# Scores and maxima of a whole chunk interleaved, and attention values summed chunk by chunk

## The chip, the cores and the metric

The kernel runs on one core of one Trainium2 chip. The metric is the device time of one execution in microseconds. Before the change three runs took 3262.71, 3264.76 and 3274.87 us; the median is 3264.76.

## The reference

Two transformer layers of the same form are applied to `x` of 4 sequences of 512 rows and 320 columns, with a context of 4 sequences of 1601 rows and 192 columns. Each layer normalises, does self-attention with 20 heads of 16 columns, normalises, does cross-attention to the context, normalises, and ends with a gated feed-forward part of 1280 hidden columns. Everything is fp32.

```python
def _attn(x, ctx, wq, wk, wv, wo, bo, heads):
    q = (x @ wq).reshape(b, n, heads, dh).transpose(0, 2, 1, 3)
    k = (ctx @ wk).reshape(b, j, heads, dh).transpose(0, 2, 1, 3)
    v = (ctx @ wv).reshape(b, j, heads, dh).transpose(0, 2, 1, 3)
    sim = jnp.einsum('bhid,bhjd->bhij', q, k) * scale
    a = jax.nn.softmax(sim, axis=-1)
    out = jnp.einsum('bhij,bhjd->bhid', a, v)
    return out.transpose(0, 2, 1, 3).reshape(b, n, heads * dh) @ wo + bo
...
x = _attn(h1, h1, ...) + x          # self: 512 keys
x = _attn(h2, context, ...) + x     # cross: 1601 keys
ff = a * jax.nn.gelu(g, approximate=False) @ ff_w2 + ff_b2
```

## The kernel before

**Units.** Attention is cut into units: one layer, one kind (self or cross), one sequence and one group of four heads. There are 20 self units and then 20 cross units in each layer, followed by four feed-forward units. A unit goes over its keys in chunks of 128: 4 chunks in a self unit, 13 in a cross unit (the last has 65 keys). So there are 160 self chunks and 520 cross chunks.

**Work of one chunk.** For each of the four heads `score` makes the transposed scores, 128 keys by 512 queries, in one PSUM bank `st`, in three passes: two products of 32 rows (queries split in a high and a low part; line 1113) and a product of 2 rows that subtracts each query's maximum (line 1116). Head j uses rows 32j to 32j+31 of TensorE, a row tile; products on different row tiles run side by side. ScalarE (ACT) then takes the exponential out of the bank into SBUF (line 1126).

**Maxima.** The maxima of a unit have to be known before its scores, so the products for them (`sps`, line 926) are made one unit ahead and stand beside the scores of the current unit: while heads 0 and 1 are scored, the maxima of heads 2 and 3 are made on the two free row tiles, and then the other way round. A bank pair holds 128 queries by 512 keys of two heads, and VectorE (DVE) reduces it (line 947). The last 65 keys of a cross unit go as a remainder of eight small passes per half (line 969). A chunk thus has two halves. `round_of` issues one half: pass by pass, the scores first, then the maxima. `give` hands out the maxima for a half; some halves get none, and some chunks get further rounds of maxima alone.

**Values.** `values` multiplies the exponentials by the values of the chunk, four heads on four column tiles (`av`, line 1141; a column of ones beside the values makes the sums). It is issued one chunk late, after the scores of the next chunk. A self unit does this for each chunk. A cross unit does it for two chunks at a time, accumulated in one bank (`n = 2 if u.cross else 1`). ACT copies the bank to SBUF (line 1157) and GpSimd (POOL) adds it to `o` (line 1158); the first copy of a unit goes straight to `o` (line 1152). The last unit before a feed-forward part has no maxima to make; it scores all four heads in one round, and there DVE adds the bank to `o` (line 1154).

**Order.** The program writes the order of each engine's queue itself. After the scores, and the late values, `steps` takes pending work from chains, by due times and a credit that each half (`tick`) adds to: query projections (line 717), keys of the context (line 779), values of the context (line 869), output projections (line 1050), normalisations. Banks come from two rings: `st`, four banks, for scores, values and most projections, and `m`, two double banks, for maxima. The exponentials and the copies of values go to SBUF places that are taken in turn (`place`, 10 in self units and 13 in cross units).

Of the kernel before, what the change touches and what calls it, by code (L numbers as in the profile page):

```python
# [64 lines left out]
def kernel(ctx: ExitStack, tc: tile.TileContext, x, context, ws, out):  # L65
# [97 lines left out]
    def place():  # L163
        these = places[at_place["kind"]]
        at_place["i"] = (at_place["i"] + 1) % len(these)
        return these[at_place["i"]]
# [184 lines left out]
    def pick():  # L351
        heads = [
            (q[0][1] + late_by(n), n)
            for n, q in chains.items()
            if q and q[0][2]() and q[0][3]() and (q[0][0][0] != LIGHT or clock["lights"])
        ]
        return min(heads)[1] if heads else None

    def run(chain):
        costs, _, ready, _, f = chains[chain].popleft()  # L360
        assert ready(), chain
        f()
        clock["credit"] -= sum(costs)
# [15 lines left out]
    def next_cost():  # L379
        name = pick()  # L380
        return None if name is None else sum(chains[name][0][0])

    def tick():
        clock["round"] += 1
        clock["credit"] = max(-2.0, min(4.0, clock["credit"] + pace()))

    def steps(beside, lights=1):


        tick()  # L390
        clock["lights"], clock["slots"] = lights, 4
        clock["tiles"] = True if beside is None else None
        done = 0
        while True:
            name = pick()
            if name is None:
                break
            cost = sum(chains[name][0][0])
            if cost >= 0.1:
                share = (2.2, 1.1) if beside else (9.0, 9.0) if beside is False else (0.5, 0.75, 1.5)  # L400
                least = cost * share[done] if done < len(share) else 3.0
                if clock["credit"] < (3.0 if beside is False else least):
                    break
                done += 1
                if clock["tiles"] is not None:
                    clock["tiles"] = name in ALIKE
            run(name)
            if cost == LIGHT:
                clock["lights"] -= 1
            clock["slots"] -= name == "slots"  # L410
        clock["tiles"] = None

    def until(test, name):
        while not test():
            assert chains[name], name
            run(name)
# [570 lines left out]
    def max_reduce(u):  # L987
        if u.pm is not None:
            nc.vector.tensor_reduce(
                u.nm.rearrange("p (j t) -> p t j", t=NQ), u.pm, AX.X, ALU.max, negate=True  # L990
            )
# [91 lines left out]
    def flush():  # L1083
        for f in late:
            f()
        late.clear()

    def round_of(scores, maxima):

        todo = [f() for f in scores] + [f() for f in maxima]  # L1090
        for i in range(max((len(passes) for passes, _ in todo), default=0)):
            for passes, _ in todo:
                if i < len(passes):
                    passes[i]()
        for _, then in todo:
            then()

    def main(u, give, nxt):

        pr = {}  # L1100
        if at_place["kind"] != u.kind:
            at_place.update(kind=u.kind, i=min(at_place["i"], len(mine) - 1))

        def score(c, j, st=None):
            r = min(P, u.nkeys - c * P)
            rows = slice(j * SLOT, (j + 1) * SLOT)
            if st is None:
                st = ps_st.tile([P, N], F32, tag="st", name="st")
            keys = u.kT[rows, u.k0 + u.cols[c] : u.k0 + u.cols[c] + r].bitcast(F32R)
            two_rows = slice(j * SLOT, j * SLOT + 2)  # L1110

            def product(e):
                nc.tensor.matmul(st[:r, :], lhsT=keys, rhs=u.q[rows, e, :].bitcast(F32R), start=(e == 0), stop=False)  # L1113

            def less_maximum():
                nc.tensor.matmul(  # L1116
                    st[:r, :],
                    lhsT=units_of[two_rows, :r].bitcast(F32R),
                    rhs=u.mrow[two_rows, :].bitcast(F32R),
                    start=False,  # L1120
                    stop=True,
                )

            def exponential():
                p = place()
                nc.scalar.activation(p[:r], st[:r], AF.Exp)  # L1126
                pr[c, j] = p

            return [lambda: product(0), lambda: product(1), less_maximum], exponential

        last = nxt is None or nxt.kind == "ff"

        def values(cs):
            if u.g in (0, 2):
                until(lambda: units[u.i - u.g].vmade[u.g // 2] > cs[-1], "values")
            ps = ps_st.tile([P, N], F32, tag="st", name="av")
            for c in cs:
                r = min(P, u.nkeys - c * P)
                for j in range(HG):
                    head = (c * H + u.g * HG + j) * VW  # L1140
                    nc.tensor.matmul(  # L1141
                        ps[j * SLOT : (j + 1) * SLOT, :],
                        lhsT=columns_of[:r, head : head + SLOT],
                        rhs=pr.pop((c, j))[:r, :],
                        start=(c == cs[0]),
                        stop=(c == cs[-1]),
                    )
            u.valued = cs[-1] + 1

            if cs[0] == 0:  # L1150
                u.o = three.tile([P, N], F32, tag="o", name="o")
                (nc.vector.tensor_copy if last else nc.scalar.copy)(u.o, ps)
            elif last:
                nc.vector.tensor_tensor(u.o, ps, u.o, ALU.add)
            else:
                vo = place()
                nc.scalar.copy(vo, ps)  # L1157
                nc.gpsimd.tensor_tensor(u.o, u.o, vo, ALU.add)  # L1158
            if u.valued == u.nch:
                add_finish(u)  # L1160


        n = 2 if u.cross else 1
        together = {min(c + n, u.nch) - 1: list(range(c, min(c + n, u.nch))) for c in range(0, u.nch, n)}

        for c in range(u.nch):
            extra = []
            if last:

                both = ps_m.tile([P, 2, N], F32, tag="m", name="st")  # L1170
                round_of([lambda j=j: score(c, j, both[:, j % 2] if j > 1 else None) for j in range(HG)], [])
                tick()
            else:
                for odd in range(2):
                    if odd:
                        tick()
                    pair, rounds = give(2 * c + odd)
                    extra += rounds
                    round_of([lambda j=j: score(c, j) for j in ((2, 3) if odd else (0, 1))], pair)
            u.scored = c + 1  # L1180

            start["both"] = True
            if extra:
                round_of([], extra[0])
            start["both"] = False
            flush()
            if c in together:
                late.append(lambda cs=together[c]: values(cs))
            steps(None, 1 if extra or c == u.nch - 1 else 2)
            for i, e in enumerate(extra[1:]):  # L1190
                if i and next_cost() is not None:
                    run(pick())
                start["both"] = True
                round_of([], e)
                start["both"] = False
            if not last and c == u.nch - 3:
                max_reduce(nxt)
                max_end(nxt)
            if loads:
                loads.popleft()()  # L1200
# [232 lines left out]
    first = units[0]  # L1433
# [22 lines left out]
    for i, u in enumerate(units):  # L1456
        nxt = units[i + 1] if i + 1 < len(units) else None
        before(u)
        if u.kind == "ff":

            flush()
            now(loads)
            loads.clear()
            until(lambda: u.hT is not None, "norm")
        add_norms(i)
        start["both"] = u.kind == "ff"
        for k in (3, AHEAD):
            v = units[i + k] if i + k < len(units) else None
            if v is not None and v.kind != "ff" and v.early == (k == AHEAD):
                add_proj(v)  # L1470
                if v.g == 0:
                    add_values(v)
        (ff_main if u.kind == "ff" else main)(u, giver(u), nxt)
# [27 lines left out]
```

## Time and profile before

| What | us |
|---|---|
| median of three runs | 3264.76 |
| profiled execution, its own time | 3267.39 |
| span of the profiled execution | 3265.6 |
| DVE, reductions for maxima `pm` (line 947) | 1127.6 busy, 980 times |
| ACT, exponentials to `pr` and `wself` (line 1126) | 947.1 and 427.6 busy |
| ACT, copies of values to `pr` (line 1157) | 140.9 busy, 236 times |
| POOL, additions of `pr` to `o` (line 1158) | 302.2 busy, 236 times |

Busy time is the union of the instructions' times on the engine. A wait is put down to the engine whose signal came last. PE is the matmul stream of TensorE, PEld its weight loads; their ends are modelled. The granted clock of TensorE was 0.967 of full speed over the span.

### The profile page before, as it was taken

How to read it: one execution, taken by the hardware profiler on the slowest of the kernel's cores; microseconds unless marked ns; L12 is line 12 of the kernel's file. 1: busy time of each engine (PE TensorE's matmuls, PEld its weight loads, DVE VectorE, ACT ScalarE, POOL GpSimd, SP SyncE). 2: the span in 40 equal slices, each digit the busy share in tenths (PEclk: the TensorE clock that was granted, in tenths of full speed). 3: DMA queues.
4: the chain of work that ended last, by engine and by line, in shares of the span. 5: the costliest groups of instructions: out<-in, count | busy, mean ns of one | idle time of the engine just before them, and what ended most of it. 6: DMA issues, size and time to landing. Idle time of an engine off the chain costs nothing.

```text
span 3265.6 us, 89144 instructions
## 1 busy us (share of the span) xinstructions
PE 3117.7 (95%) x36690; PEld 1686.7 (52%) x36690; DVE 2077.9 (64%) x2833; ACT 1866.6 (57%) x3721; POOL 972.6 (30%) x1141
## 2 busy tenths in 40 slices
PE   7899899999999999999998998999999999999999
PEld 3455455555455555455444554555555555554555
DVE  6766777777777776522246777777777777774221
ACT  3666566776667676711126665667767777765110
POOL 2435232323323332111114453324233333322000
PEclk8999899999999999999989998999999999999999
DMA  3433222211212211200113332212112111112000
GB/s 92 91 65 77 44 43 45 54 39 38 65 33 42 60 35 28 80 4 6 27 23 73 72 62 44 41 40 51 33 39 55 36 41 39 39 22 65 9 10 15
DMA packets 213039, 145.08 MB, mean 44 GB/s; under 512 B 65556, under 2 KB 203160, under 8 KB 212632
## 3 DMA queue, kind: packets, MB, share of 16 engines
q1 hardware_dynamic: 211368, 138.32, 19.1%
q8 instruction: 289, 4.73, 0.6%
q10 hardware_dynamic: 1264, 1.06, 0.1%
q14 instruction: 118, 0.97, 0.1%
HBM read 33.04 MB, written 7.93 MB: 13 GB/s over the span
## 4 chain that ended last, share of the span: by engine, by line
PE 80%; DVE 8%; ACT 4%; issue 3%; DMA 2%; SPq 2%; POOL 1%; ACTq 0%; DVEq 0%; POOLq 0%
PE av L1141 19%; PE st L1113 19%; PE fps L1246 9%; PE st L1116 6%; PE yps L1302 5%; PE sps L926 5%; DVE pm L947 3%; PE kps L779 3%; PE qps L717 3%; PE vps L869 3%; PE ops L1050 3%; DVE nmax L947 2%; PE fps L1259 2%; ACT pr L1126 2%; PE kps L749 1%
## 5 line engine op out<-in xcount | busy, mean ns | idle before, releaser
L947 DVE TENSOR_REDUCE pm<-sps 128x2 f32<-128x1024 f32 (+1 forms) x980 | 1127.6, 1195 | 225.3 <-PE sps L926 199.6
L1113 PE MATMUL st<-q,kT 32*128 32x512 f32 (+1 forms) x5440 | 1089.3, 445 | 40.5 <-DVE x L1057 8.0
L1126 ACT ACTIVATE pr<-st 128x512 f32<-128x512 f32 (+1 forms) x1791 | 947.1, 602 | 269.9 <-PE st L1116 252.1
L926 PE MATMUL sps<-kT,q 32*128 32x512 f32 (+1 forms) x6400 | 993.6, 411 | 52.9 <-DMA kT<-stage 20.1
L1113 PEld LDWEIGHTS st<-q,kT 32*128 32x128 f32 (+1 forms) x5440 | 537.6, 182 | 482.3 <-ACT pr L1126 160.2
L1116 PE MATMUL st<-m,units 2*128 2x512 f32 (+1 forms) x2720 | 655.3, 400 | 5.9 <-issue 2.1
L1141 PE MATMUL av<-pr,vals 128*32 128x512 f32 (+1 forms) x3582 | 644.5, 636 | 16.9 <-ACT pr L1126 10.3
L1158 POOL TENSOR_TENSOR o<-o,pr 128x512 f32<-128x512 f32 x236 | 302.2, 1281 | 951.2 <-ACT pr L1157 931.2
L926 PEld LDWEIGHTS sps<-kT,q 32*128 32x128 f32 x6400 | 474.1, 188 | 103.6 <-DVE pm L947 33.3
L947 DVE TENSOR_REDUCE nmax<-sps 128x2 f32<-128x1024 f32 (+1 forms) x356 | 381.2, 1109 | 175.2 <-PE sps L926 121.6
L1126 ACT ACTIVATE wself<-st 128x512 f32<-128x512 f32 (+1 forms) x801 | 427.6, 602 | 75.1 <-PE st L1116 68.6
L1116 PEld LDWEIGHTS st<-m,units 2*128 2x128 f32 (+1 forms) x2720 | 350.7, 184 | 42.8 <-issue 7.7
L1141 PE MATMUL av<-wself,vals 128*32 128x512 f32 (+1 forms) x1602 | 344.5, 635 | 3.6 <-ACT pr L1126 3.0
L1246 PE MATMUL fps<-hT,w 128*128 128x512 f32 x640 | 285.4, 599 | 1.8 <-DVE pr L1272 0.9
L1269 ACT ACTIVATE pr<-fps,b 128x512 f32<-128x512 f32 x80 | 50.6, 683 | 370.4 <-PE fps L1259 268.1
L1141 PEld LDWEIGHTS av<-pr,vals 128*32 128x32 f32 (+1 forms) x3582 | 114.3, 112 | 236.9 <-issue 101.4
L1158 POOL TENSOR_TENSOR o<-o,wself 128x512 f32<-128x512 f32 x89 | 114.0, 1281 | 381.5 <-ACT wself L1157 381.5
L1157 ACT COPY pr<-av 128x512 f32<-128x512 f32 x236 | 140.9, 597 | 135.7 <-PE av L1141 134.7
L1246 PEld LDWEIGHTS fps<-hT,w 128*128 128x128 f32 x640 | 118.9, 190 | 151.8 <-issue 146.6
L624 POOL TENSOR_SCALAR stage<-stage 128x256 fp32r<-128x256 f32 (+1 forms) x155 | 107.1, 691 | 218.6 <-ACT stage L725 135.5
L624 POOL TENSOR_SCALAR w<-w 128x896 fp32r<-128x896 f32 x40 | 98.1, 2452 | 147.0 <-DVE w L789 118.5
L1050 PE MATMUL ops<-wo,aT 112*32 112x160 f32 (+1 forms) x3072 | 128.5, 303 | 4.1 <-ACT pr L1126 2.8
(100 smaller groups left out, 3020.8 us busy)
## 6 DMA issues: line engine op xcount, KB each, us to landing
kT<-w SPq DMA_DIRECT2D x160, 192.0 KB
q<-stage SPq DMA_DIRECT2D x320, 64.0 KB
q<-stage SPq DMA_DIRECT2D x154, 128.0 KB
aT<-o SPq DMA_DIRECT2D x320, 32.0 KB
m<-turned SPq DMA_DIRECT2D x636, 2.0 KB
kT<-stage SPq DMA_DIRECT2D x156, 64.0 KB
w<-in_L_xattn_ff_w_dram SPq DMA_DIRECT2D x20, 256.0 KB
ctxT<-ctxT SPq DMA_DIRECT2D x24, 208.0 KB
```

The source lines that it names most:

```text
L624: eng.tensor_scalar(high.bitcast(F32R), x, 1.0, None, ALU.mult)
L926: nc.tensor.matmul(out, lhsT=u.q[rows, e, queries].bitcast(F32R), rhs=u.kT[rows, keys].bitcast(F32R), start=(e == 0), stop=(e == 1),)
L947: nc.vector.tensor_reduce(to[:, j : j + n], part, AX.X, ALU.max, negate=(ns == 1))
L1050: nc.tensor.matmul(ps[f : f + m, : D // 2], lhsT=aT[:n, k, t * P + f : t * P + f + m], rhs=wo[:n, k, cols], start=(k == 0), stop=(k == 2),)
L1113: nc.tensor.matmul(st[:r, :], lhsT=keys, rhs=u.q[rows, e, :].bitcast(F32R), start=(e == 0), stop=False)
L1116: nc.tensor.matmul(st[:r, :], lhsT=units_of[two_rows, :r].bitcast(F32R), rhs=u.mrow[two_rows, :].bitcast(F32R), start=False, stop=True,)
L1126: nc.scalar.activation(p[:r], st[:r], AF.Exp)
L1141: nc.tensor.matmul(ps[j * SLOT : (j + 1) * SLOT, :], lhsT=columns_of[:r, head : head + SLOT], rhs=pr.pop((c, j))[:r, :], start=(c == cs[0] ...
L1157: nc.scalar.copy(vo, ps)
L1158: nc.gpsimd.tensor_tensor(u.o, u.o, vo, ALU.add)
L1246: nc.tensor.matmul(ps, lhsT=w1[:, k, i * FF + c * P : i * FF + (c + 1) * P], rhs=u.hT[:, k, :], start=ahead and k == 0, stop=not ahead and ...
L1302: nc.tensor.matmul(ps[:, :D], lhsT=hid[c][:, t * P : (t + 1) * P], rhs=w2[:, c, :], start=(c == 0), stop=(c == NHC - 1),)
```

## The change

The two halves of a chunk are collected first and handed to a new function `side_by_side`. It makes two lists of passes: the scores of heads 0 and 1 followed by the maxima of the same heads, and the maxima of heads 2 and 3 followed by their scores. The lists are issued in step, so that each step has one product on each of the four row tiles. Where the second list's maxima are a remainder, its scores go first. The exponentials and reductions are issued after all products, in the order as before. `n` becomes 1, so a cross unit too multiplies, copies and adds the values of each chunk by itself.

```diff
+    def side_by_side(halves):
+        tiles = []
+        for odd, (scores, maxima) in enumerate(halves):
+            tiles.append(([p for p, _ in scores], [p for passes, _ in maxima for p in passes]))
+        (s0, m0), (s1, m1) = tiles
+        first = [[p[i] for p in s0] for i in range(3)] + [[p] for p in m1]
+        second = [[p[i] for p in s1] for i in range(3)]
+        long = len(m0) > 2
+        second = second + [[p] for p in m0] if long else [[p] for p in m0] + second
+        for i in range(max(len(first), len(second))):
+            for tile in (first, second):
+                for p in tile[i] if i < len(tile) else ():
+                    p()
+        for scores, maxima in halves:
+            for _, then in scores + maxima:
+                then()
...
-        n = 2 if u.cross else 1
+        n = 1
         together = {min(c + n, u.nch) - 1: list(range(c, min(c + n, u.nch))) for c in range(0, u.nch, n)}
...
             else:
+                halves = []
                 for odd in range(2):
                     if odd:
                         tick()
                     pair, rounds = give(2 * c + odd)
                     extra += rounds
-                    round_of([lambda j=j: score(c, j) for j in ((2, 3) if odd else (0, 1))], pair)
+                    halves.append(([score(c, j) for j in ((2, 3) if odd else (0, 1))], [f() for f in pair]))
+                side_by_side(halves)
             u.scored = c + 1
```

## The prediction

> **What bounds the kernel now.** I read the page's table of engines first, then the stage windows, then the waits of one stage, then the timeline of single chunks.
>
> ```profile
> PE 3117.7 (95%) x36690; PEld 1686.7 (52%) x36690; DVE 2077.9 (64%) x2833; ACT 1866.6 (57%) x3721; POOL 972.6 (30%) x1141
> ```
>
> PE looks full, but the ends of matmuls are modelled, so this is no proof. The windows split the span by stage; here are the two stretches of cross-attention, without the last unit of each (us, then busy time and instructions of each engine, PE clock, DMA share, GB/s):
>
> ```profile
> 453.00:1353.00 900.00, 874.67 (x11926) 482.52 (x11921) 660.19 (x810) 626.88 (x1259) 280.49 (x274) 0.97 0.20 43
> ...
> 2082.00:2957.00 875.00, 857.12 (x11924) 476.37 (x11917) 653.32 (x766) 626.31 (x1257) 282.04 (x274) 0.98 0.18 39
> ```
>
> These 1775 us hold 38 units of 13 chunks. DVE is busy 74% there, ACT 71%, POOL 32%: no other engine is the bound on average. The waits of weight loads in the first stretch show what holds PE (us in total, times, longest):
>
> ```profile
> PEld st L1113 <- ACT pr L1126: 70.2, 153, 0.8
> PEld st L1113 <- ACT wself L1126: 44.8, 96, 0.8
> PEld av L1141 <- ACT pr L1126: 36.9, 81, 0.8
> ```
>
> Score products wait for a bank of the four-bank ring, which an exponential on ACT has to empty; waits of maxima products for DVE are smaller (13.4 us). The timeline shows the place: two cross chunks with no projection beside them, PE and ACT rows picked:
>
> ```profile
> 1326.98 0.50 PE L1113 MATMUL st<-q,kT 32*128 32x512 f32 x2
> ...
> 1328.69 0.98 PE L1113 MATMUL st<-q,kT 32*128 32x512 f32 x2
> ...
> 1330.05 2.08 ACT L1126 ACTIVATE wself<-st 128x512 f32<-128x512 f32 x4
> ...
> 1331.05 0.62 PE L1141 MATMUL av<-wself,vals 128*32 128x512 f32 x1
> ...
> 1332.90 0.50 PE L1113 MATMUL st<-q,kT 32*128 32x512 f32 x2
> ```
>
> The odd chunk, which has no value products, takes 1.71 us (1326.98 to 1328.69). The even one, with value products of two chunks, takes 4.21: its scores stand still while ACT empties the eight banks of both chunks, and then ACT idles while 16 value matmuls run. The pair takes 5.92 us. The eight exponentials run from 1328.04 to 1332.13, 0.51 each, and the copy of the values takes 0.58, so ACT works 4.7 of it. Work is bunched: first PE waits for ACT, then ACT for PE.
>
> The self-attention stage already does one chunk's values at a time. One of its chunks without a projection:
>
> ```profile
> 1950.69 0.49 PE L1113 MATMUL st<-q,kT 32*128 32x512 f32 x2
> ...
> 1952.40 1.06 PE L1141 MATMUL av<-pr,vals 128*32 128x512 f32 x8 [0.27 <-ACT pr L1126]
> ...
> 1953.39 0.50 PE L1113 MATMUL st<-q,kT 32*128 32x512 f32 x2
> ```
>
> It takes 2.70 us (1950.69 to 1953.39), with four exponentials and one copy in ACT's queue. At 0.51 and 0.58 these are 2.6 us of ACT, so this rhythm leaves it almost no gap. The first chunk of a cross unit also has one value group; the 27 without a projection have a median of 2.73.
>
> **The change, part by part.**
>
> *Five groups.* Before, the order of passes in a chunk is already: first scores with maxima twice, subtraction, second scores with maxima twice, subtraction. The first pair's subtraction is directly followed by the second pair's first product, which uses the other two row tiles, and where no bank is waited for they start together (both at 1951.26 in the self chunk). So the fifth group is shared already. In the instruction order of the two programs, 611 of the 680 chunks issue the same PE sequence. Only 69 differ: those in which the first half has no maxima, or has the 65-key remainder. There all eight score products now go before the rest. One group takes 0.23 us (1951.03 to 1951.26, the second and third step of the self chunk); a gain or loss of one group in 69 chunks is 16 us either way. I take 0, since the four scores together also need four free banks at once. SP's queue issues the same 2070 instructions in the same order.
>
> *Values one chunk at a time* acts in the 38 cross units. PE issues the same number of value matmuls. Added are 228 copies on ACT and 228 additions on POOL, six per unit, at the mean times of these rows of the page:
>
> ```profile
> L1158 POOL TENSOR_TENSOR o<-o,pr 128x512 f32<-128x512 f32 x236 | 302.2, 1281 | 951.2 <-ACT pr L1157 931.2
> ...
> L1157 ACT COPY pr<-av 128x512 f32<-128x512 f32 x236 | 140.9, 597 | 135.7 <-PE av L1141 134.7
> ```
>
> That is 136 us of ACT and 292 us of POOL. Whether ACT's share costs time is read per pair of chunks (odd, then even; six pairs in each of 38 units, 228; the 38 first chunks keep their one group). I took from the trace the time from each chunk's first score product to the next's, sorted by the projection that falls in it, and used medians. After, a bare chunk is 2.70. One with a query projection is 1.71 until the values, 0.84 of values, 0.77 of projection (907.66 to 908.43 in the timeline): 3.3. One with an output projection is 3.5 (fastest self row 3.52). One with a block of values is 1.71 + 0.84 + 1.6 = 4.2, where 1.6 is the block's price in a chunk without values (3.34 less 1.71). One with keys of the context is 5.42, a row that exists (11 first chunks).
>
> - 62 pairs with nothing beside: 5.94 becomes 5.40, gain 0.54, 33 us.
> - 38 with one query projection: 24 at 6.60 and 14 at 6.10 become 6.0: 16 us.
> - 42 with one block of values: 7.3 to 7.8 becomes 6.9; 0.5 each: 22 us.
> - 22 with keys of the context: 8.17 (15) and 8.37 (7) become 8.12: 2 us.
> - 26 with one output projection: 14 at 6.24 and 12 at 6.94 become 6.2: 9 us.
> - 38 with more than that: PE is the limit in both chunks, 0.3 each as a middle between 0 and the bare 0.54: 12 us.
>
> Together 94 us. From below: only bare pairs gain, 33 us. From above: every pair gains what bare pairs do (123 us), and the stalls that bare pairs' mean (6.55) has over their median shrink by half (62 × 0.3 = 19): some 140 us.
>
> The rows behind ACT's added copy are the next chunk's exponentials; the bank it frees is needed by that chunk's fourth score. This wait is inside the 2.70. The place that POOL's addition reads is written again 13 places later, over two chunks on; behind it in POOL's queue stand the splits of keys and queries, which can be 1.28 us later, and behind these SP's moves. POOL's load becomes (563 + 292) of about 1680 us, 51%. Waits of PE for moved keys are 20.1 us in all now; I put 0 on it and keep +20 for the range. DVE gets nothing in these units; its reductions (four in a row took 4.62 beside the cross pair shown, 2.31 per chunk) fit in 2.70 with 0.39 left, so unit ends, which add transposes and a division there, will stall PE about as now.
>
> *The two last units* (26 chunks) do their additions on DVE: 12 more at 0.69 us, 8 us. Their pairs take 3.35 + 0.80 = 4.15 now, eight exponentials at 0.5; ACT stays the limit. I take 0, with 8 as the bound.
>
> Sum: the profiled execution's own time is 3267.4 (span 3265.6). Less 94 it is 3173. The median shown, 3264.8, lies 2.6 lower, so I predict **3171 us**.
>
> **A rule weighed.** The row is ACT's 71% in the cross stretches. The Trainium skill, TensorEngine Tiling (Array Packing), section PSUM Bottleneck, says that tiling speeds up TensorE but not the emptying of PSUM, and that the copies out may become the bottleneck after a fourfold speedup. This speaks against more copies: if all 228 land on the path, the sum would be +136 us, about 3401. The trace here agrees that PE waits for ACT's emptying, but shows the copies falling into idle time of ACT in chunks with one value group.
>
> **The rivals.**
>
> 1. *ACT becomes the bound* (slower). A copy more per two chunks lengthens ACT's queue, and the fourth score waits for it. It decides where a bare one-value chunk exceeds 2.97 us, half of today's 5.94. For it: laden chunks of self-attention exceed my values in the mean (output projection 4.18 against 3.52). Against: 2.70 and 2.73. If each copy costs its full 0.597, 3401; if half, 3333.
> 2. *DVE eats the gain* (about the same). With 2.31 of 2.70 taken and two banks for maxima, every extra DVE piece would stop PE. DVE in these units is 1313 us; to give 94 us its idle time has to shrink from 461 to 367. For it: waits of products for reductions exist (13.4 us). Against: 74% busy becomes only 78%. Time: 3265 less the 33 of bare pairs at most, so 3232 to 3265.
> 3. *The groups really save a group in each chunk* (faster still). 654 × 0.23 = 150 more, 3020. Against: the order of PE is the same in 611 chunks, so this cannot be but for the 69.
> 4. *The change does nothing*: this is what I expect of the self stages; it would hold for the whole only if the added copies cost just what the smoothing saves, 3265.
>
> **How the numbers follow.** Forecast's mechanism, with its own range 3115 to 3235: 0.68. More than that, by stalls that go too or the third rival: 0.05. Within 0.5% (16 us, about what a measurement here tells from no change): 0.10, second and fourth rival. Slower by the first rival, partly or in full: 0.15. What the mechanism leaves between 3235 and 3248 is 0.02. So faster 0.75, same 0.10, slower 0.15. The range for 8 in 10 reaches from 3095, where the 69 chunks and the upper bound of the pairs join, to 3290, which takes in the second rival and the mildest part of the first.
>
> **What would show it.** Score products in the order named, with two subtractions and first products of the other pair sharing a start. ACT copies of values 576 instead of 348, POOL's row the same count, PE's matmuls unchanged. Bare cross chunks all near 2.7 instead of 1.7 and 4.2. The cross stretches of 900 and 875 us shorter by about 47 each; self stages and feed-forward unchanged. Waits of score products for ACT smaller in total, ACT near 80% in the cross stretch. I am wrong if bare cross chunks take over 2.97, if laden chunks lose more than bare ones gain, or if waits for reductions or for POOL appear ahead of score products.

## The result, and the profile after

The kernel after the change takes 3283.92 us (median of 20 runs, 3264.83 to 3292.42); the kernel before, run beside it, 3266.65 (20 runs, 3257.66 to 3277.35). The ratio is 1.0044, with a 95% interval of 1.003 to 1.0057: 0.44% slower, where 3171 us was forecast. The profiled execution has a span of 3282.8 us, against 3265.6.

The page's engine table and its rows for the copy of a value bank and for POOL's addition (for a row: times, then busy us and mean ns of one, then idle time before it):

```profile
PE 3092.3 (94%) x36690; PEld 1648.6 (50%) x36690; DVE 2107.8 (64%) x2845; ACT 1960.4 (60%) x3949; POOL 1262.7 (38%) x1369
...
L1177 POOL TENSOR_TENSOR o<-o,pr 128x512 f32<-128x512 f32 x376 | 482.1, 1282 | 804.6 <-ACT pr L1176 756.3
...
L1176 ACT COPY pr<-av 128x512 f32<-128x512 f32 x376 | 227.3, 605 | 42.5 <-PE av L1160 40.5
```

What the change adds is as counted: 228 more instructions on ACT and on POOL, 12 on DVE, none on PE, and POOL's additions cost 1.28 us each as before. (The new function moves lines: score products are now L1132, subtractions L1135, exponentials L1145, value products L1160.) The windows of the two cross-attention stretches (us, length, then busy time and instructions of PE, PEld, DVE, ACT, POOL, the granted clock, DMA share, GB/s):

```profile
460.00:1361.00 901.00, 856.11 (x11926) 466.26 (x11925) 673.00 (x810) 673.30 (x1373) 426.35 (x388) 0.97 0.19 43
...
2095.00:2973.00 878.00, 838.87 (x11904) 455.74 (x11898) 662.33 (x766) 671.73 (x1368) 426.28 (x387) 0.98 0.18 39
```

They are 901 and 878 us long, against 900 and 875: the 47 us forecast in each are not there, yet no engine has become full. ACT is at 76% there (71 before), DVE at 75 (74), POOL at 48 (32). PE is busy 18 us less in each, so it waits more. Its waits in the first stretch (us in total, times, longest), the answer to the three lines shown of before:

```profile
PEld st L1132 <- ACT pr L1145: 71.9, 94, 1.7
...
PEld av L1160 <- ACT pr L1145: 64.3, 128, 1.0
...
PEld st L1132 <- ACT wself L1145: 49.8, 63, 1.7
...
PE st L1135 <- DMA m<-turned: 8.1, 8, 1.3
```

Score products wait about as long for their banks as before (121.7 us against 115.0), in far fewer and longer waits, up to 1.7 us instead of 0.8; a wait of subtractions for moved maxima (`m<-turned`) has appeared. But the mechanism of the forecast is there too. This is the timeline of the same pair of chunks whose 5.92 us the prediction showed:

```profile
1335.10 0.50 PE L1132 MATMUL st<-q,kT 32*128 32x512 f32 x2
...
1335.29 0.61 ACT L1176 COPY wself<-av 128x512 f32<-128x512 f32 x1
...
1336.16 1.09 ACT L1145 ACTIVATE wself<-st 128x512 f32<-128x512 f32 x2 [0.26 <-PE st L1135]
...
1337.84 0.50 PE L1132 MATMUL st<-q,kT 32*128 32x512 f32 x2
...
1340.64 0.50 PE L1132 MATMUL st<-q,kT 32*128 32x512 f32 x2
```

The chunks take 2.74 and 2.80 us, 5.54 for the pair, with ACT idle 0.2 to 0.3 in each. A gain of 0.38 in this pair is real; something else gave it back.

### The profile page after: what moved, and what is told of

It reads as the page before. It is cut to its first block, busy times and chain, and to the rows that moved or that the text cites. A ratio compares the mean times of both kernels' runs of the same rounds, so it can differ in the third digit from the quotient of the medians.

```text
span 3282.8 us, 90045 instructions
## 1 busy us (share of the span) xinstructions
PE 3092.3 (94%) x36690; PEld 1648.6 (50%) x36690; DVE 2107.8 (64%) x2845; ACT 1960.4 (60%) x3949; POOL 1262.7 (38%) x1369
## 3 DMA queue, kind: packets, MB, share of 16 engines
q14 instruction: 126, 1.03, 0.1%
## 4 chain that ended last, share of the span: by engine, by line
PE 73%; DVE 11%; ACT 5%; issue 3%; SPq 3%; DMA 2%; POOL 2%; ACTq 0%; DVEq 0%; POOLq 0%
PE av L1160 17%; PE st L1132 16%; PE fps L1267 9%; PE st L1135 5%; PE yps L1323 5%; DVE pm L947 5%; PE sps L926 4%; PE kps L779 3%; PE vps L869 3%; PE qps L717 3%; ACT pr L1145 3%; DVE nmax L947 2%; SPq L1006 2%; PE ops L1050 2%; PE fps L1280 2%
## 5 line engine op out<-in xcount | busy, mean ns | idle before, releaser
L1145 ACT ACTIVATE pr<-st 128x512 f32<-128x512 f32 (+1 forms) x1792 | 947.2, 602 | 312.5 <-PE st L1135 298.4
L1132 PE MATMUL st<-q,kT 32*128 32x512 f32 (+1 forms) x5440 | 1009.5, 448 | 34.2 <-DVE nmax L947 7.2
L1177 POOL TENSOR_TENSOR o<-o,pr 128x512 f32<-128x512 f32 x376 | 482.1, 1282 | 804.6 <-ACT pr L1176 756.3
L1132 PEld LDWEIGHTS st<-q,kT 32*128 32x128 f32 (+1 forms) x5440 | 503.4, 184 | 517.3 <-ACT pr L1145 170.2
L1160 PE MATMUL av<-pr,vals 128*32 128x512 f32 (+1 forms) x3584 | 670.2, 634 | 37.5 <-ACT pr L1145 18.5
L1135 PE MATMUL st<-m,units 2*128 2x512 f32 (+1 forms) x2720 | 599.1, 403 | 23.7 <-DMA m<-turned 20.1
L1145 ACT ACTIVATE wself<-st 128x512 f32<-128x512 f32 (+1 forms) x801 | 428.1, 603 | 102.7 <-PE st L1135 95.8
L1160 PE MATMUL av<-wself,vals 128*32 128x512 f32 (+1 forms) x1602 | 348.4, 616 | 13.9 <-ACT pr L1145 13.5
L1177 POOL TENSOR_TENSOR o<-o,wself 128x512 f32<-128x512 f32 x176 | 225.9, 1283 | 323.0 <-ACT wself L1176 315.7
L1135 PEld LDWEIGHTS st<-m,units 2*128 2x128 f32 (+1 forms) x2720 | 311.0, 185 | 69.9 <-issue 28.3
L1176 ACT COPY pr<-av 128x512 f32<-128x512 f32 x376 | 227.3, 605 | 42.5 <-PE av L1160 40.5
L1160 PEld LDWEIGHTS av<-pr,vals 128*32 128x32 f32 (+1 forms) x3584 | 93.6, 109 | 210.1 <-ACT pr L1145 103.2
L1050 PEld LDWEIGHTS ops<-wo,aT 112*32 112x32 f32 (+1 forms) x3072 | 99.8, 112 | 66.7 <-issue 31.5
```

Source lines behind the costliest of these rows:

```text
L1050: nc.tensor.matmul(ps[f : f + m, : D // 2], lhsT=aT[:n, k, t * P + f : t * P + f + m], rhs=wo[:n, k, cols], start=(k == 0), stop=(k == 2),)
L1135: nc.tensor.matmul(st[:r, :], lhsT=units_of[two_rows, :r].bitcast(F32R), rhs=u.mrow[two_rows, :].bitcast(F32R), start=False, stop=True,)
L1160: nc.tensor.matmul(ps[j * SLOT : (j + 1) * SLOT, :], lhsT=columns_of[:r, head : head + SLOT], rhs=pr.pop((c, j))[:r, :], start=(c == cs[0] ...
```

## Experiments

Two questions were put: which of the two edits loses, and where. Times of chunks below are, as in the prediction, from a chunk's first score product to the next one's, out of the profiled executions. The kernels of the first group ran beside a kernel before at 3270.15 us, those of the second at 3272.78, of the third at 3274.59; ratios are to these.

**One edit at a time.** `inter` keeps the new order of products and multiplies values two chunks at a time:

```diff
# the kernel after
-        n = 1
+        n = 2 if u.cross else 1
```

> The changed kernel with values two chunks at a time in cross units again, so only the grouping of score and maxima products is left of the change. Theory A (the values one by one bring the loss: they leave DVE and the maxima of the next unit no slack): the grouping costs only what the self stages and the remainder chunks show after the change, 3266 to 3282. Theory B (the grouping is the loss and hides a gain of the values): 3320 or more, since the values' gain is then about 50 or more.

`n1` is the opposite: the old order, with values one chunk at a time.

```diff
# the kernel before
-        n = 2 if u.cross else 1
+        n = 1
```

> The kernel before with values one chunk at a time in cross units, the grouping left out. Theory A: 3260 to 3275, the self stages as before, chunks 0 of cross units long as after the change (4.4 instead of 3.6). Theory B: 3220 or less, with bare pairs at 5.4 and chunks 0 at 3.6.

Measured: `inter` 3343.75 us, ratio 1.0228 [1.02, 1.0257]; `n1` 3226.37 us, ratio 0.9864 [0.9838, 0.9891]. So the values gain 44 us and the order of products, which was costed at nothing, loses 74 alone, and 58 on top of the values (59 by the ratios). `inter` is as theory B had it. `n1` fits neither theory as a whole: its time is near B's, but its first chunks of cross units take 4.61 us, near what A had said, and not 3.6. Where the order loses is read chunk by chunk. The instruction order differs in 69 chunks: 38 cross chunks where the first half's maxima are the 65-key remainder (chunk 10 of a unit), and 31 chunks where the first half has no maxima. The sums in us:

| Chunks | before | inter | n1 | after |
|---|---|---|---|---|
| 38 with the remainder | 181.8 | 236.1 | 125.5 | 149.8 |
| 31 without first maxima | 136.0 | 153.0 | 139.6 | 158.1 |
| 68 that follow the 38 | 260.0 | 259.9 | 222.8 | 238.8 |
| 38 first chunks of cross units | 136.4 | 139.1 | 175.2 | 170.6 |

(The first row is an even chunk, with two value groups in before and inter, one in n1 and after. The third leaves out eight that belong to the second.) Inter loses 71.3 us in the 69 chunks, of 77.2 between the spans. After against n1, 62.9 between the spans, it loses 24.3 and 18.5 in them and 16.0 in the chunks behind.

The timelines of one such chunk show how. First n1, chunk 10 of a cross unit of the second layer (start, length, then in brackets the idle time before):

```profile
2498.73 0.49 PE L1113 MATMUL st<-q,kT 32*128 32x512 f32 x2
...
2499.30 0.39 PE L1116 MATMUL st<-m,units 2*128 2x512 f32 x2
...
2499.78 2.07 ACT L1126 ACTIVATE pr<-st 128x512 f32<-128x512 f32 x4 [0.27 <-PE st L1116]
...
2499.88 0.71 DVE L969 TENSOR_REDUCE pm<-sps 128x8 f32<-128x528 f32 x1 [1.33 <-PE sps L926]
...
2501.53 0.50 PE L1113 MATMUL st<-q,kT 32*128 32x512 f32 x2
```

The same chunk in the kernel after:

```profile
2546.84 1.56 PE L1132 MATMUL st<-q,kT 32*128 32x512 f32 x8
...
2547.67 0.29 PEld L1132 LDWEIGHTS st<-q,kT 32*128 32x128 f32 x5 [0.31 <-ACT pr L1176]
...
2548.01 0.62 PE L1135 MATMUL st<-m,units 2*128 2x512 f32 x4
...
2548.25 1.19 PE L926 MATMUL sps<-kT,q 32*128 32x512 f32 x20
2548.50 2.06 ACT L1145 ACTIVATE pr<-st 128x512 f32<-128x512 f32 x4 [0.89 <-PE st L1135]
...
2549.48 0.71 DVE L969 TENSOR_REDUCE pm<-sps 128x8 f32<-128x528 f32 x1 [2.82 <-PE sps L926]
...
2550.37 0.50 PE L1132 MATMUL st<-q,kT 32*128 32x512 f32 x2
```

In n1 the first pair's subtraction comes 0.57 us after the chunk's start, and ACT has its first exponential 0.48 later. In after the eight score products go first, and the last of them waits for the last of four banks, which ACT's copy of the values empties; the subtractions of both pairs stand behind it, 1.17 us in. ACT has nothing to do for 0.89 us instead of 0.27. The twenty products for maxima, which used to fill the wait for banks, come last; DVE idles 2.82 us instead of 1.33. The chunk takes 3.53 instead of 2.80 us, and 0.62 of these 0.73 are ACT's added idle time. Over all 69 chunks the two traces give the same picture: in after the first subtraction comes 0.60 us later than in n1 in the mean, and ACT idles 40 us longer, of the 43 us that these chunks lose. The clock has little part in it: 37 of the 38 chunks and 21 of the 31 run at a granted clock of 1.0 in both kernels, and they lose 0.61 and 0.41 us each.

In inter, where the values are not yet in small pieces, the loss in the 38 is 1.43 us per chunk. ACT's queue before the last bank is longer there, but this is not all: by the trace's records of the clock, the 38 chunks hold 86 us at half speed (a granted clock of 0.5), against 19 in before. The 18 of them that run at a clock of 1.0 in both kernels lose 0.39 us each, the other 20 lose 2.4.

**The loss in the 38 undone.** `after_long` orders only these 38 chunks as before:

```diff
# the kernel after
-                side_by_side(halves)
+                if len(halves[0][1]) and len(halves[0][1][0][0]) > 2:
+                    for scores, maxima in halves:
+                        round_of([lambda s=s: s for s in scores], [lambda m=m: m for m in maxima])
+                else:
+                    side_by_side(halves)
```

> The changed kernel with the 38 chunks that have the 65-key remainder in their first half ordered as before; only the 31 chunks without maxima in the first half keep the new order. If the remainder chunks are the larger part of the grouping's loss (24 us in them and about 15 in the two chunks after, by the two traces): 3240 to 3250. If the 31 chunks are (18 us by the traces): 3265 or more.

Measured: 3249.52 us, ratio 0.9929 [0.9903, 0.9956]. The 38 chunks are back at 125.5 us and those behind at 223.2. That is 34 us of the 58 (38 of the 59 by the ratios); the 31 chunks without first maxima still cost 156.5, which is 17 more than in n1, and account for most of what is left (n1's ratio is 0.9864).

**DVE.** The rival that DVE eats the gain was tested by giving DVE less to do in both kernels. The full reductions for maxima go over 256 of the 512 keys, so half of those keys are left out of the maxima:

```diff
-                    nc.vector.tensor_reduce(to[:, j : j + n], part, AX.X, ALU.max, negate=(ns == 1))
+                    nc.vector.tensor_reduce(to[:, j : j + n], part[:, :, :256], AX.X, ALU.max, negate=(ns == 1))
```

In the kernel before:

> The kernel before with reductions over 256 of the 512 keys of each bank (the other half of the maxima is left out), so one takes about 0.65 us less 0.05 instead of 1.19. It is the base for the next kernel. If DVE is not what holds the kernel before: 3230 to 3260. If it is: 3150 or less.

In the kernel after:

> The changed kernel with reductions over 256 of the 512 keys (the other half of the maxima is left out). Theory A, DVE being full in one-value chunks: it gains much more by this than the kernel before does, and lies 60 to 100 us under the kernel before with the same cut. If DVE has no part: it stays 10 to 25 us above it.

Measured: 3187.66 and 3188.24 us, ratios 0.9745 [0.9708, 0.9781] and 0.9745 [0.9717, 0.9772]. The engine table of the lighter kernel before:

```profile
PE 3070.8 (96%) x36690; PEld 1675.4 (53%) x36690; DVE 1458.1 (46%) x2833; ACT 1861.3 (58%) x3721; POOL 971.1 (30%) x1141
```

and of the lighter kernel after:

```profile
PE 3045.5 (95%) x36690; PEld 1638.3 (51%) x36690; DVE 1469.2 (46%) x2845; ACT 1955.1 (61%) x3949; POOL 1260.8 (40%) x1369
```

DVE falls from 64% to 46% of the span in both, but the two lie 0.6 us apart, where the theory of DVE wanted the kernel after 60 to 100 us lower. Without any part of DVE it was expected 10 to 25 us higher, as the full kernels lie 17 apart. So at most some 17 us are left for DVE, about the spread of the four runs of each light kernel, and DVE does not eat a gain of 94. The lighter kernel before lies between the two times expected for it: the reductions do hold it in part, by a way that was not followed up.

**The first chunks.** In n1 the chunks 1 to 12 of the 38 cross units gain 81 us (43.10 to 40.97 us per unit), and the first chunks lose 39 of it (3.59 to 4.61 us each). The waits of the whole run name what they wait for: the rows of maxima, which SP's queue moves from `turned` to `m` (line 1006). Of before:

```profile
PEld st L1116 <- DMA m<-turned: 3.9, 5, 1.6
...
PE st L1116 <- DMA m<-turned: 1.7, 3, 1.2
```

Of n1:

```profile
PE st L1116 <- DMA m<-turned: 16.4, 18, 1.5
...
PEld st L1116 <- DMA m<-turned: 5.5, 5, 1.5
```

And n1's timeline of the end of one unit and the start of the next (SPq is SP's queue of moves):

```profile
2460.28 0.21 DVE L1000 STREAM_TRANSPOSE turned<-nm 128x32 f32<-128x32 f32 x1
...
2460.55 4.63 SPq L1006 DMA_DIRECT2D m<-turned  x8
...
2464.93 0.50 PE L1113 MATMUL st<-q,kT 32*128 32x512 f32 x2
...
2466.49 0.50 PE L1116 MATMUL st<-m,units 2*128 2x512 f32 x2 [0.83 <-DMA m<-turned]
```

The last reduction of the next unit's maxima is handed out in chunk 10; the chain behind it on DVE ends at 2460.49, in chunk 11. Then SP issues eight moves, 0.58 us each, and the rows are there some 6 us after the chain's end. Chunks 11 and 12, which have to cover this, took 2.19 + 5.20 = 7.4 us in the mean before, and take 3.13 + 3.32 = 6.45 in n1. Counted from the chain's end to the next unit's first score product, it is 6.73 us in the mean before and 5.07 in n1; the first subtraction comes 0.57 us after that product where nothing delays it. That the smoother units no longer cover the moves was tested in three ways. `n1_norow` leaves the moves out in all cross units but the first of each layer (`u.early`; the expectation of `before_norow` calls the units concerned "not scored alone", which is not what the edit tests). Those units subtract an earlier unit's maxima.

```diff
# n1
-                queue.dma_start(out=to[i, e], in_=turned[rows, :])
+                if not u.cross or u.early:
+                    queue.dma_start(out=to[i, e], in_=turned[rows, :])
```

> Values one chunk at a time with the products ordered as before, and the moves of the maxima to their rows left out in cross units (the old rows are used). Theory C (the first chunk of a cross unit, 4.61 us instead of 3.59, waits for these eight moves, which now have 6.4 instead of 7.4 us of chunks 11 and 12 to hide in): first chunks back at 3.6 or less, about 39 us less than with values one at a time alone, 3180 to 3195. Theory D (the first chunks are long because ACT or DVE is full at a unit's end): first chunks stay above 4.2, 3215 or more.

`n1_early` finishes the maxima of cross units one chunk earlier; the two constants of the planner that hand out the maxima (4 halves before the end) become 6.

```diff
# n1
-            if not last and c == u.nch - 3:
+            if not last and c == u.nch - (4 if u.cross else 3):
                 max_reduce(nxt)
                 max_end(nxt)
...
-                rest = v.start - (7 if alone else 4) - clock["round"]
+                rest = v.start - (7 if alone else 6 if u.cross else 4) - clock["round"]
...
-                if not hand and ahead[0].start - 4 - clock["round"] > 1:
+                if not hand and ahead[0].start - (6 if u.cross else 4) - clock["round"] > 1:
```

> Values one chunk at a time, products ordered as before, and in cross units the maxima of the next unit are finished one chunk earlier, so the moves have three chunks. Theory C: the wait is gone, less some 5 to 20 us for one more round of maxima alone per unit: 3190 to 3215. Theory D: 3225 or more, since the same work is only moved.

`n1_split` lets POOL's queue issue four of the eight moves:

```diff
# n1
-                queue = (nc.sync, nc.scalar)[e] if start["on"] else nc.sync
+                queue = (nc.sync, nc.scalar)[e] if start["on"] else (nc.sync, nc.gpsimd)[i % 2] if u.cross else nc.sync
```

> Values one chunk at a time, products ordered as before, and in cross units every second of the eight moves of maxima is issued by POOL instead of SP, so SP's 4.6 us of issues become 2.3. Theory C: first chunks near 3.6 to 3.9 and 3190 to 3210, if POOL's additions and splits behind the waiting moves cost nothing. Theory D: 3225 or more.

Measured, beside n1's 3226.37 and 0.9864:

| Kernel | us | ratio | first chunk, mean | chunks 1 to 12, sum |
|---|---|---|---|---|
| n1_norow | 3192.96 | 0.976 [0.9734, 0.9785] | 3.80 | 40.92 |
| n1_early | 3233.69 | 0.988 [0.9856, 0.9904] | 3.83 | 41.86 |
| n1_split | 3213.64 | 0.982 [0.9791, 0.9849] | 4.02 | 41.14 |

Without the moves, 33 us go, and 31 of them are in first chunks (0.81 × 38). Finishing earlier takes the first chunk's loss away as well, but pays it elsewhere: 0.28, 0.49 and 0.37 us more in chunks 4, 8 and 9, where the maxima now have to be squeezed in, so it gains nothing: the time that theory D expected, but not D's reason, since the first chunks did fall. With two queues each queue's issues take half as long, as a unit's moves in n1_split's timeline show; POOL's start as an addition ends, so that all eight are out after 3.2 us instead of 4.6. First chunks and time stay a little above what theory C expected (3.9 and 3210), but this is the fastest of the complete kernels, 59 us (1.8%) under the kernel before beside it:

```profile
2458.62 2.37 SPq L1006 DMA_DIRECT2D m<-turned  x4
...
2459.56 2.29 POOL L1006 DMA_DIRECT2D m<-turned  x4
```

The wait itself is only a part of what the late rows cost. Waits of products and weight loads for them sum to 21.9 us in n1, against 5.6 in before. But by the trace's records of the clock, the first two chunks of the 38 units also hold 61 us at half speed in n1, against 2 in before and 19 in n1_norow. An estimate from these: if PE sets the pace there, half of the added 59 us is lost time, up to 30 us. It fits that the 11 first chunks with keys of the context beside them lose 2.3 us each and the 27 without a projection 0.5. No run separates wait and clock.

**The same moves left out of the other two kernels**, to see whether leaving them out helps any kernel, and whether the order of products loses its time within its chunks or by making these rows late. The edit is that of n1_norow.

> The kernel before, with the moves of the rows of maxima left out in the cross units that are not scored alone (their maxima are then those of an earlier unit, the work is otherwise the same). Theory C, the wait of a unit's first chunk for the moved rows is made by the one-chunk values: before waits for these moves 5.6 us in all, products and weight loads together, so leaving them out gives at most 10 us, 3256 to 3266. Rival R, leaving out the moves helps any kernel by itself, by freeing SP's queue: some 30 us as in the one-chunk form, 3230 to 3240.

> The kernel after, with the same moves left out. Theory C: after waits 28 us for these moves and lost about 39 us in its first chunks, so 3240 to 3260. If the five groups' loss in the 69 chunks comes only through the later rows of the next unit, more than that goes, to 3195 to 3225, near the one-chunk form without the moves (3193); if it is lost within the chunk itself, the two forms stay 40 us or more apart, so 3235 or above.

Measured: 3266.32 us, ratio 0.9987 [0.9966, 1.0008], and 3238.43 us, ratio 0.99 [0.9867, 0.9933]. In before the moves cost nothing, so theory R falls: the two-chunk rhythm hides them, and the change to one chunk uncovers them. In after, leaving them out saves 45 us by the medians; its first chunks go from 4.49 to 3.57 us, 35 us in all, and the time at half speed in the first two chunks from 53 to 9 us. Its waits for maxima rows were

```profile
PE st L1135 <- DMA m<-turned: 20.1, 20, 1.5
...
PEld st L1135 <- DMA m<-turned: 8.2, 7, 1.5
```

and are 3.7 and 1.4 us without the moves. But after without the moves still stands 45 us over n1 without them (3238 against 3193), and its 38 remainder chunks take 149.3 us, as with them: the order of products loses its time inside its chunks and the next two, not by way of the rows.

So the sum, from the spans: 81 us gained in chunks 1 to 12, 39 lost in the first chunks, some 4 gained elsewhere, and then 63 lost by the order of products. That gives 17 slower, which is the difference between the two spans.

## Why the prediction was wrong

It failed in two of its steps.

*Five groups, "I take 0".* The 69 chunks were found, and so was the reason why they might lose ("the four scores together also need four free banks at once"), but the price was taken from the wrong row: one group of products, 0.23 us per chunk, 16 us either way. What changes in these chunks is not the number of groups. It is when ACT gets its first bank, and what PE does while it waits for the last. In inter the chunks lose 1.03 us each (71.3 / 69), the time at half speed included, and in after 0.62 (42.8 / 69), with 16.0 us more in the chunks behind. The row to take was ACT's emptying of a bank, 0.51 us per exponential: the first subtraction now stands behind the products for all four banks, where before it needed only the first two. By this estimate, which is made with the result known, one to two emptyings, 0.5 to 1.0 us, for each of 69 chunks, the step would have read 35 to 70 us.

*Values one chunk at a time, −94 us.* The pairs were right in kind and nearly in size: they give 81 us in n1. Bare pairs have a median of 5.55 us in n1, in place of 5.40. By kind, n1 gained 44 on bare pairs (33 forecast), 24 on those with a block of values (22), 9 on query projections (16), 9 on output projections (9), and lost 2 on keys of the context (gain 2) and 3 on laden ones (gain 12). Of the pairs with keys, three run 5.4 to 6.8 us at half speed and lose 6 us together; most others gain. That laden pairs gain nothing because PE is the limit there was not tested. The order of products takes most of it away again: in after the bare pairs' gain is 10. What failed is the sentence that "the 38 first chunks keep their one group". Their own work is unchanged, but they need the rows of maxima, whose chain did not get shorter: the shortest seen from its last DVE operation to the first subtraction is about 5.8 us, eight issues of 0.58 and the landing of the last. The two chunks that hid it did get shorter. The prediction looked at SP's moves only as followers of POOL (+20 us); the chain from DVE's last reduction over SP to the next unit's first subtraction was not laid beside the two chunks before it. First chunks cost 39 us more in n1 and 34 in after. Of POOL's load itself nothing was seen to stop PE.

The rest of the steps: *the two last units* were costed at 0 with 8 as the bound, and their 24 chunks take 2.1 us more. DVE's additions there rose from 12 to 24 at 0.69, as said. *Self stages unchanged*: the 137 of their chunks with the old order went from 694.9 to 692.8, right; the 23 others lost 13.7, which belongs to the first step.

The rivals. *ACT becomes the bound* did not come true: where the order of products is unchanged, bare chunks stayed at 2.74 to 2.80 in the pair shown (in n1 the median pair takes 5.55), under its 2.97, and ACT is at 76% in the cross stretches, less than the 80% forecast; the ACT rows' union grew by 46 us in a stretch for 114 copies, 0.4 each, since neighbours on ACT overlap (four exponentials of 0.60 us each take 2.06 together). The prediction had also weighed a rule of the Trainium skill, TensorEngine Tiling (Array Packing), section PSUM Bottleneck: the copies out of PSUM may become the bottleneck. With all 228 copies on the path the sum was +136 us, and the runs went against it as far as the copies go: n1 has all of them and is 44 us faster. The rule's thought, that the banks' emptying sets the pace, was right in the place where it was not applied, at the four banks of the 69 chunks. *DVE eats the gain*: its upper end, 3265, is as near to the result as any rival's time, but the two light kernels leave its mechanism 17 us at most. *The groups really save* has the sign wrong. *Nothing changes* comes within 0.6% of the time for a wrong reason: a gain of 44 us and a loss of 58 that nearly cancel. That the result lies inside the range named for 8 in 10, 3095 to 3290, is luck: its upper end was put there for the second rival and the mildest part of the first, and neither is what happened.

## What to carry to other kernels

Price a re-ordered product not by its own length but by the engine behind it: ask when the consumer gets its first full buffer, and what fills the producer's wait for the last free one. When a loop is made shorter or smoother, look up what ran beside it unseen: a fixed chain of moves (here 5.8 us, against a cover of 7.3 before and 5.6 in n1, both counted from the end of the last DVE operation) becomes a wait as soon as its cover falls under it, and then the remedy is at the chain. Two edits that come together are worth running one by one even when the sum is near zero: here one alone is 1.4% faster than the kernel before, and with the issues of the moves split over two queues 1.8%.

## What the runs showed of the hardware that was not expected

*A wait of little more than a microsecond can be followed by half speed.* In after, a first chunk with keys of the context waits 1.21 us for its rows. Windows of that stretch (the wait, the chunk's scores and values, then the keys in two parts; the granted clock is the number behind POOL's busy time):

```profile
892.50:894.00 1.50, 0.29 (x8) 0.12 (x5) 1.24 (x2) 0.24 (x1) 1.11 (x1) 1.00 0.02 3
894.00:896.10 2.10, 1.86 (x20) 0.59 (x20) 1.18 (x1) 1.62 (x4) 0.14 (x1) 1.00 0.00 0
896.10:898.00 1.90, 1.90 (x52) 1.69 (x56) 0.04 (x1) 0.92 (x2) 0.83 (x1) 0.62 0.03 9
898.00:900.20 2.20, 2.20 (x56) 1.60 (x40) 0.00 (x0) 0.00 (x0) 0.43 (x1) 0.56 0.00 0
```

The granted clock falls to 0.62 and 0.56 while PE is fully busy, and the 96 matmuls of the keys take 4.21 us, where the same ones in before, at a clock of 1.00, took 2.53. The Trainium skill, TensorE: Matmul & The Clock Gate, section What's actually happening, puts the throttling at one idle window or more of about 3.4 us; here PE's longest idle stretch in the 6 us before was 1.21 us, and the clock fell all the same, 2.6 us after that stretch had ended, for 3.41 us by the trace's record. Over the run, the trace's records of the clock give 216 us at half speed before, 203 in n1, 235 in after and 320 in inter. Of the 103 us that inter has more than before, 67 are in the 38 chunks with the remainder. So part of what inter lost can be clock; how much, no run here separates.

*A small DVE operation can wait out a POOL addition.* The rounding of the maxima (line 998, 128 by 16) has a median of 0.17 us in both kernels, but in after's timeline there is:

```profile
932.89 1.29 POOL L1177 TENSOR_TENSOR o<-o,pr 128x512 f32<-128x512 f32 x1 [2.25 <-ACT pr L1176]
...
933.08 1.13 DVE L998 TENSOR_SCALAR nm<-nmax 128x16 fp32r<-128x16 f32 x1
```

It ended with the addition (934.18 and 934.21). Its mean rose from 267 ns before to 413 in after (277 in n1), 11.7 us over its 80 instructions, and it stands in the chain of the rows. All 26 of the 80 that take over 0.25 us in after end within 0.04 us of a POOL addition that was running when they started (14 in before, 14 in n1). As n1 has the same number of additions as after, it is their timing and not their number that made the difference. The Trainium skill, SBUF — State Buffer, section SBUF: two separate sides, describes such an exclusive lock between certain DVE operations and GpSimd, held for a whole instruction; these rows agree with it, and the reductions out of PSUM beside additions kept their 1.19 us.

*DVE's reductions matter more than their share says.* Halved reductions brought both kernels to 2.5% under the kernel before, with DVE busy only 64% of the span there. Which of its waits that took away was not followed up; the time at half speed fell too, from 216 to 161 us in before and from 235 to 154 in after.
